# A planned two-layer graph attention kernel: other landing times and another search in its planner, and W2's column sums without score columns

## The chip, the cores and the metric

The kernel runs on one core of a Trainium2 chip. The metric is the device time of one execution in microseconds (us). A core has five engines that matter here: TensorE (PE, matrix products into PSUM), VectorE (DVE), ScalarE (ACT), GpSimd (POOL) and SyncE (SP). Each works off its own list of instructions in order; an instruction that has to wait for a semaphore holds up everything behind it on the same engine. In this kernel SP issues the plain and transposing DMAs, and POOL issues the DMAs that add to their destination.

## The reference

For 32 graphs of 512 nodes with 512 features, the reference normalizes x, applies two graph attention layers with the same 0/1 adjacency mask, and adds the result to x. The first layer has 4 heads of 256 features and an ELU, the second has one head of 512.

```python
def gat_layer(x, mask, W, a_src, a_dst, bias, concat):
    xl = (x @ W).reshape(B, N, H, F)
    asrc = jnp.einsum('bnhf,hf->bnh', xl, a_src)
    adst = jnp.einsum('bnhf,hf->bnh', xl, a_dst)
    e = jax.nn.leaky_relu(asrc[:, :, None, :] + adst[:, None, :, :], 0.2)
    e = jnp.where(mask[..., None], e, -1e9)
    attn = jax.nn.softmax(e, axis=1)
    out = jnp.einsum('bsdh,bshf->bdhf', attn, xl)
    return (out.reshape(B, N, H * F) if concat else out.mean(axis=2)) + bias

h = jnp.maximum(_layernorm(x, axis=-1), 0.0)
h1 = jax.nn.elu(gat_layer(h, mask, W1, att_src1, att_dst1, b1, concat=True))
out = x + gat_layer(h1, mask, W2, att_src2, att_dst2, b2, concat=False)
```

## The kernel before

**The work of one batch.** A batch (one graph) goes through five stages. `load` and `norm` bring x in and normalize it; `norm_turn` transposes it into `ht`. `project1` multiplies `ht` by W1 into `xl`, with two extra columns per head that hold the two attention scores of each node. For each head, `Soft.columns`, `Soft.first` and `Soft.second` make the attention weights: the scores are turned and sent as a row to DRAM and back to all partitions (tiles `as`, DRAM `das`), ScalarE makes the leaky ReLU and the exponentials (tile `l`), VectorE the masked minimum, a second row goes the same way (tiles `rr`, DRAM `drr`), VectorE builds `p` from it, POOL adds the mask to `p` with an accumulating DMA (`p<-dm`), and ScalarE takes the exponential of `p`. `gather1` multiplies by `xl` into `h1`; `elu` follows. `project2` multiplies `h1` by W2 into `xl2`, and `gather2` multiplies by the second layer's `p` and adds x. Products use a seven-product scheme for two-by-two blocks (as Strassen's), so VectorE also makes sums and differences of blocks (`hs`, `t`, `hl`, in-place ones), and each of seven products is emptied from its PSUM bank by ScalarE (a copy) or VectorE (an add or subtract) before the next product may be put into the bank.

**The order of the work.** Nothing is emitted when these functions run. Each call adds a job to a `Program`: its engine, a cost in us, the tiles it reads and writes, and for DMAs a size in us of transfer. `Program.order` then plans. TensorE's jobs keep the order in which the code adds them. For the other four engines a simulation (`forwards`) takes, whenever an engine is free, the ready job with the lowest rank. A DMA is held to have landed `DMA_LEAD` + its size (divided by a speed if both queues transfer) + `DMA_TAIL` after its issue; `DMA_TAIL` is 1.2 us for both queues. A DMA is not issued while more than `AHEAD` = 3.5 us of transfers are queued. Twelve rounds of a backwards and a forwards simulation give ranks, and the best round is kept. Then, for stretches of 80 TensorE jobs (`STRETCH`), `sooner` lowers the rank of jobs that stand in the chain of causes before a TensorE gap, in one of six `WAYS` (how far back, how strongly), and the whole program is simulated again; a try is kept if TensorE comes to a job 40 beyond the stretch sooner. Each engine's jobs are emitted in the planned order, which is then fixed.

**W2 and the second bias.** Layer 1's output is kept one higher than ELU gives it, so the column sums of W2 are taken from the bias once. `weights2` is called in the code after the first batches' projections. It loads W2 as four blocks (`w2_sb`, 512 KB each), b1, b2 and the two score vectors of layer 2 (spread over all partitions, into two `t` tiles); the four W2 loads read the key of `ht`'s first tile, so they wait for the last job that wrote it, which at that place is batch 1's `norm_turn`. Then VectorE multiplies every row of W2 with each score vector and sums: 2 vectors x 4 blocks x 4 = 32 products, whose sums land in `part`, and four small adds put them into column 256 of each block (`w2s`). `bias2` multiplies a tile of ones by the blocks, 257 columns wide (two PSUM banks of eight program-level matmuls each, 32 matmul instructions in the trace), subtracts the banks from `b2_sb`, takes `c2` (the scores' offset) from column 256, and sets that column to 0. On TensorE the job of `bias2` stands between batch 1's `project1` and batch 0's gathers. `b2_sb` is read by `project2` as the first content of its banks, `c2` by `scores_2`.

In the trace, W1 and W2 both show as `w_sb`, the DVE jobs have line L449, the ACT jobs L446, the matmuls L463, the DMAs of SP L452 (L658 and L717 for the two kinds of transposes), those of POOL L457. DVE accumulations show as a product and a short read of the accumulator.

Of the kernel before, what the change touches and what calls it, by code (L numbers as in the profile page):

```python
# [3 lines left out]

# [6 lines left out]
F32 = mybir.dt.float32  # L11
# [4 lines left out]
OP = mybir.AluOpType  # L16
# [3 lines left out]
P = 128  # L20
# [5 lines left out]
def rows_of(ap, n):  # L26

    return bass.AP(tensor=ap.tensor, offset=ap.offset, ap=[[0, n], [1, ap.shape[-1]]])
# [31 lines left out]
        self.free.append(key[1])  # L60


class Program:


# [4 lines left out]

    CROSS, SAME = 0.15, 0.07
    PAIRS = {("PE", "ACT"): 0.21, ("PE", "DVE"): 0.21, ("DVE", "POOL"): 0.58, ("POOL", "DVE"): 0.4}
    DMA_LEAD, DMA_TAIL, AHEAD = {"SP": 0.6, "POOL": 0.75}, {"SP": 1.2, "POOL": 1.2}, 3.5
    ALONE = {"SP": 1.0, "POOL": 1.0}
    SHARED = {0: {"SP": 0.44, "POOL": 0.62}, 1: {"SP": 0.3, "POOL": 0.62}}
    TURN = 0.95
# [90 lines left out]
                release(j, lambda s: t + jobs[j][1] + self.latency(j, s))  # L167
        return start, done, cause

    def sooner(self, rank, start, cause, span, gain, first, last):  # L170


        jobs, lost, free = self.jobs, {}, 0.0
        for i, j in enumerate(self.tensor):
            gap, free = start[j] - free, start[j] + jobs[j][1]
            if not first <= i < last:
                continue
            d = cause[j]
            while gap > 0.05 and d is not None and start[j] - start[d] < span:
                lost[d] = max(lost.get(d, 0.0), gap)  # L180
                d = cause[d]
        return [r - gain * lost.get(j, 0.0) for j, r in enumerate(rank)]

    WAYS = tuple((span, gain) for span in (60.0, 25.0) for gain in (2.0, 0.7, 6.0))
    STRETCH = 80

    def backwards(self, rank):

# [60 lines left out]
    def order(self):  # L249
        jobs = self.jobs  # L250
        n = len(jobs)
        self.after = [[] for _ in range(n)]
        for j, job in enumerate(jobs):
            for d in job[2]:
                self.after[d].append(j)

        need, pe = [0.0] * n, None
        for j in reversed(range(n)):
            later = self.DMA_LEAD.get(jobs[j][0], 0.0) + self.DMA_TAIL.get(jobs[j][0], 0.0) + (jobs[j][4] or 0.0)
            need[j] = max(  # L260
                (
                    need[s] + jobs[s][1] + (later if jobs[j][4] is not None else self.latency(j, s))
                    for s in self.after[j]
                ),
                default=0.0,
            )
            if jobs[j][0] == "PE":
                if pe is not None:
                    need[j] = max(need[j], need[pe] + jobs[pe][1])
                pe = j  # L270
        best, self.tried = None, []
        self.tensor = [j for j in range(n) if jobs[j][0] == "PE"]

        def look(rank):
            nonlocal best
            start, done, cause = self.forwards(rank)
            end = max(start[j] + jobs[j][1] for j in range(n))
            self.tried.append(end)
            if best is None or end < best[0]:
                best = end, start, done, cause, rank  # L280
            return start, cause

        rank = need
        for _ in range(self.ROUNDS):
            back = self.backwards(rank)
            rank = [-back[j] - jobs[j][1] for j in range(n)]
            start, cause = look(rank)
            rank = [-start[j] - jobs[j][1] for j in range(n)]

        _, start, done, cause, rank = best  # L290
        n_pe = len(self.tensor)
        for first in range(0, n_pe, self.STRETCH):
            last = min(first + self.STRETCH, n_pe)
            goal = self.tensor[min(last + self.STRETCH // 2, n_pe - 1)]
            tries = deque(self.WAYS)
            while tries:
                new = self.sooner(rank, start, cause, *tries.popleft(), first, last)
                if new == rank:
                    break
                result = self.forwards(new)  # L300
                if result[0][goal] < start[goal] - 0.01:
                    rank, (start, done, cause) = new, result
                    tries = deque(self.WAYS)
                    self.tried.append(max(start[j] + jobs[j][1] for j in range(n)))
        self.start, self.late = start, rank
        return done

    def emit(self):
        for j in self.order():
# [4 lines left out]
def tile_gat(  # L314
# [36 lines left out]
    nc = tc.nc  # L351
# [10 lines left out]
    KH = FT // 2  # L362
    W2H = DO // 2 + 1
    assert N == 512 and D == 512 and DO == D and FH == 256 and H == 4

    sbuf = ctx.enter_context(tc.tile_pool(name="sbuf", bufs=1))
# [22 lines left out]
    AT = {(0, 0): 0, (0, 1): 6, (1, 0): 1, (1, 1): 2}  # L389
    b1_sb = sbuf.tile([P, FT], F32, name="b1_sb")  # L390
    b2_sb = sbuf.tile([P, 2, W2H], F32, name="b2_sb")
    c2 = sbuf.tile([P, 2], F32, name="c2")
    w1_low = sbuf.tile([P, 3, W], F32, name="w1_low")
    hl = sbuf.tile([P, 3, P], F32, name="hl")
    later = sbuf.tile([P, 2, W], F32, name="later")
# [52 lines left out]
    def dve(cost, reads, writes, f, *a, **k):  # L448
        prog.add("DVE", cost, reads, writes, lambda: f(*a, **k))  # L449

    def dma(size, reads, writes, to, at, cost=0.4):
        prog.add("SP", cost, reads, writes, lambda: nc.sync.dma_start(to, at), size)  # L452
# [100 lines left out]
                prog.alias(vk + (u, c), [vk + ("v", a, j) for a in range(2) for j in range(H // 2)])  # L553
        ps_.give(vk)

    def weights2():

        for (r, c), ix in AT.items():
            dma(
                1.5, [("ht", 0, 0)], [("w2", ix)], w2_sb[:, ix, :, :M],  # L560
                w2[r * HF // 2 : (r + 1) * HF // 2, c * DO // 2 : (c + 1) * DO // 2].rearrange(
                    "(k p) f -> p k f", p=P
                ),
            )
        dma(0.1, (), ["b1"], b1_sb, b1.rearrange("(c p) -> p c", p=P))
        dve(TINY, ["b1"], ["b1"], nc.vector.tensor_scalar_add, b1_sb, b1_sb, 1.0)
        dve(0.3, (), ["b2"], nc.vector.memset, b2_sb, 0.0)
        for c in range(2):
            dma(
                0.4, (), ["b2"], b2_sb[:, c, :M],  # L570
                bass.AP(tensor=b2.tensor, offset=b2.offset + c * M, ap=[[0, P], [1, M]]),
            )
        for a, v in enumerate((as2, ad2)):
            lk, bc = ts_.take()
            dma(0.75, (), [lk], bc, rows_of(v[0], P))
            for (r, c), ix in AT.items():
                for k in range(KH):
                    jk, junk = xrs.take()
                    dve(
                        0.4, [lk, ("w2", ix)], [("part", a, r, c, k), jk],  # L580
                        nc.vector.scalar_tensor_tensor,
                        junk[:, : DO // 2], w2_sb[:, ix, k, :M], 1.0,
                        bc[:, c * DO // 2 : (c + 1) * DO // 2], op0=OP.mult, op1=OP.mult,
                        accum_out=part[:, a, r * KH + k, c : c + 1],
                    )
                    xrs.give(jk)
            ts_.give(lk)
        for a in range(2):
            for r in range(2):
                g = part[:, a, r * KH : (r + 1) * KH, :]  # L590
                dve(
                    TINY, [("part", a, r, c, k) for c in range(2) for k in range(KH)],
                    [("w2s", AT[r, a])], nc.vector.tensor_add,
                    w2_sb[:, AT[r, a], :, M:], g[:, :, 0:1], g[:, :, 1:2],
                )


    def bias2():

        ok, ones = ts_.take()  # L600
        ones = ones[:, :P]
        dve(0.2, (), [ok], nc.vector.memset, ones, 1.0)
        for c in range(2):
            bk, bt = banks.take(W2H)
            pe(
                [ok, *(k for r in range(2) for k in (("w2", AT[r, c]), ("w2s", AT[r, c])))],
                [bk], 2 * KH * W2H / 593,
                [
                    (mm, (bt[:, :W2H], ones, w2_sb[:, AT[r, c], k, :]),
                     dict(start=(r == 0 and k == 0), stop=(r == 1 and k == KH - 1)))  # L610
                    for r in range(2) for k in range(KH)
                ],
            )
            dve(ADD, [bk, "b2"], ["b2"], nc.vector.tensor_sub, b2_sb[:, c], b2_sb[:, c], bt[:, :W2H])
            banks.give(bk)
        dve(TINY, ["b2"], ["c2"], nc.vector.tensor_copy, c2, b2_sb[:, :, M])
        dve(0.34, ["b2"], ["b2"], nc.vector.tensor_sub, b2_sb[:, 1], b2_sb[:, 1], b2_sb[:, 0])
        dve(TINY, ["b2", "c2"], ["b2"], nc.vector.memset, b2_sb[:, :, M:], 0.0)
        ts_.give(ok)

    XT, MASK, MASKT, ST = {}, {}, {}, {}
# [789 lines left out]
    def run(products):  # L1411
        for _ in products:
            pass
# [18 lines left out]
    scores1()  # L1432
    masks(0)
    given = [zs.take() for _ in range(2)]
    run(project1_first(given))
    load(1)
    norm(1)
# [143 lines left out]
```

## Time and profile before

| what | value |
|---|---|
| time, median of 3 runs (lowest to highest) | 2785.98 us (2781.57 to 2786.17) |
| the profiled execution's own time | 2789.86 us |
| span of that execution, first to last instruction | 2788.1 us |
| mean granted TensorE clock | 0.999 |
| first matmul starts | 10.6 us |
| ACT busy | 2244.9 us (81%) |
| POOL busy | 328.0 us (12%) |
| DMA: bytes moved, mean rate | 502.09 MB, 180 GB/s |
| accumulating DMAs p<-dm | 314, 512 KB each |
| relays as<-das and rr<-drr | 96 and 161 |

The profile page comes from one execution. Busy time counts an engine's instructions from start to end; the ends of matmuls are modelled. A wait is put down to the engine, or the landing of a DMA, whose semaphore event came last before the waiting instruction started. In the rows below, a row of a timeline gives the start in us, the time in us that the merged instructions took together, the engine, the line, the operation, what is written and read, the shape, how many instructions were merged, and in brackets the idle time before and who ended it. A row of waits gives who waited for whom, the total in us, how often, and the longest in us. A row of a stage gives its time, then for PE, PEld (weight loads), DVE, ACT and POOL the busy time and the number of instructions, then the granted clock, the DMA engines' busy share and GB/s.

### The profile page before, as it was taken

What the parts mean: (1) busy time and instruction counts of PE and PEld (TensorE: products, weight loads), DVE (VectorE), ACT (ScalarE), POOL (GpSimd) and SP (SyncE); (2) the same over time, 40 slices, a digit from 0 to 9 for tenths busy, and PEclk for the clock granted to TensorE, in tenths of its full rate; (3) what the DMA queues carried; (4) which work ended last, traced back from release to release, by engine and by line L of the source; (5) the groups of instructions that cost most, each with busy time, mean ns of one, the idle gap of its engine ahead of it and who ended that gap; (6) DMA issues with size and microseconds to landing.
All of it is one profiled execution on the core that took longest, in us unless ns stands there. A gap on an engine that the chain in (4) does not pass through costs nothing. (4 is left out here: it accounts for less than half of the span.)

```text
span 2788.1 us, 41716 instructions
## 1 busy us (share of the span) xinstructions
PE 2747.0 (99%) x12490; PEld 2361.8 (85%) x12490; DVE 2626.0 (94%) x6857; ACT 2244.9 (81%) x4751; POOL 328.0 (12%) x356
## 2 busy tenths in 40 slices
PE   8999999999999999999999999999999999999999
PEld 7688888888888888888888888888888888888877
DVE  8989999999999999999999999999999999999986
ACT  5978887888888888978788887878878788788873
POOL 0100111101111101111011111111110111101110
PEclk9999999999999999999999999999999999999999
DMA  7766767676776677666676766776666876677663
GB/s 237 154 170 176 205 168 191 183 184 177 192 187 173 182 183 200 172 173 182 167 200 172 192 179 185 167 196 184 171 188 171 197 178 170 177 184 197 167 167 106
DMA packets 375861, 502.09 MB, mean 180 GB/s; under 512 B 222804, under 2 KB 227668, under 8 KB 375636
## 3 DMA queue, kind: packets, MB, share of 16 engines
q1 hardware_dynamic: 329844, 332.68, 42.9%
q0 software_dynamic: 45792, 166.74, 25.2%
q8 instruction: 100, 1.64, 0.2%
q14 instruction: 125, 1.02, 0.1%
HBM read 316.41 MB, written 51.31 MB: 132 GB/s over the span
## 5 line engine op out<-in xcount | busy, mean ns | idle before, releaser
L463 PE MATMUL mm<-w_sb,hs 128*128 128x257 f32 (+2 forms) x3032 | 697.5, 381 | 3.8 <-DVE hs L449 1.9
L463 PEld LDWEIGHTS mm<-w_sb,hs 128*128 128x128 f32 x3032 | 574.5, 190 | 91.4 <-DVE hs L449 3.1
L457 POOL DMA_DIRECT2D p<-dm x314 | 275.6, 878 | 2306.4 <-DVE p L449 1212.1
L446 ACT ACTIVATE l<-as,z 128x512 f32<-128x512 f32 x640 | 439.9, 716 | 111.6 <-DMA as<-das 110.4
L446 ACT ACTIVATE l<-l,low 128x512 f32<-128x512 f32 x640 | 457.5, 718 | 34.4 <-DVE low L449 32.2
L446 ACT ACTIVATE p<-p,z 128x512 f32<-128x512 f32 (+1 forms) x636 | 430.9, 715 | 56.3 <-DMA p<-dm 45.8
L463 PE MATMUL mm<-w_sb,h 128*128 128x257 f32 x2056 | 469.4, 380 | 3.8 <-ACT w_sb L446 3.8
L463 PE MATMUL mm<-p,xl 128*128 128x256 f32 (+1 forms) x1984 | 468.0, 384 | 1.5 <-ACT h L446 1.5
L449 DVE SCALAR_TENSOR_TENSOR p<-rr,z 128x512 f32<-128x512 f32 (+1 forms) x636 | 447.6, 738 | 16.2 <-DMA rr<-drr 15.9
L449 DVE CUSTOM_DVE_ANT_1 l<-l,mt 128x512 f32<-128x512 f32 x640 | 426.1, 681 | 21.4 <-ACT l L446 20.6
L463 PEld LDWEIGHTS mm<-w_sb,h 128*128 128x128 f32 x2056 | 389.7, 190 | 62.5 <-ACT w_sb L446 4.2
L463 PE MATMUL mm<-w_sb,ht 128*128 128x258 f32 x1802 | 428.9, 385 | 13.8 <-DVE xl L449 12.6
L463 PEld LDWEIGHTS mm<-p,xl 128*128 128x128 f32 x1984 | 377.1, 190 | 62.0 <-issue 6.0
L463 PEld LDWEIGHTS mm<-w_sb,ht 128*128 128x128 f32 x1802 | 336.9, 190 | 80.2 <-DVE xl L449 29.7
L446 ACT ACTIVATE h<-mm,b_sb 128x256 f32<-128x256 f32 (+1 forms) x504 | 232.0, 474 | 144.7 <-PE mm L463 142.7
L446 ACT ACTIVATE xl<-mm 128x258 f32<-128x258 f32 (+2 forms) x686 | 253.8, 379 | 50.6 <-PE mm L463 47.8
L449 DVE TENSOR_TENSOR xl<-xl,mm 128x258 f32<-128x258 f32 (+1 forms) x526 | 212.4, 414 | 38.0 <-PE mm L463 29.2
L463 PE MATMUL mm<-t,hs 128*128 128x256 f32 x992 | 225.5, 379 | 0.1
L463 PEld LDWEIGHTS mm<-t,hs 128*128 128x128 f32 x992 | 188.2, 190 | 26.6 <-ACT h L446 0.6
L446 ACT ACTIVATE xr<-h 128x512 f32<-128x512 f32 x256 | 159.2, 627 | 40.8 <-DVE h L449 39.2
L449 DVE TENSOR_TENSOR t<-mm,t 128x256 f32<-128x256 f32 (+1 forms) x424 | 171.7, 416 | 15.3 <-PE mm L463 13.7
L463 PE MATMUL mm<-xl,p 128*128 128x256 f32 (+1 forms) x752 | 179.3, 387 | 0.0
(130 smaller groups left out, 3448.2 us busy)
## 6 DMA issues: line engine op xcount, KB each, us to landing
p<-dm POOLq DMA_DIRECT2D x314, 512.0 KB, 5.6
rr<-drr SPq DMA_DIRECT2D x159, 512.0 KB
x<-in_x_dram SPq DMA_DIRECT2D x129, 256.0 KB
adj<-in_adj_dram SPq DMA_DIRECT2D x128, 256.0 KB
as<-das SPq DMA_DIRECT2D x64, 512.0 KB
t<-in_x_dram SPq DMA_DIRECT2D x124, 256.0 KB
out_dram<-t SPq DMA_DIRECT2D x124, 256.0 KB
dm<-m SPq DMA_DIRECT2D x64, 256.0 KB
```

The costliest lines, as they stand in the source:

```text
L446: prog.add("ACT", cost, reads, writes, lambda: nc.scalar.activation(*a, **k))
L449: prog.add("DVE", cost, reads, writes, lambda: f(*a, **k))
L457: lambda: nc.gpsimd.dma_start(to, at, accum_op=OP.add), size,
L463: f(*a, **k)
```

## The change

It has three parts.

1. `DMA_TAIL` is 2.7 us in place of 1.2 us. In the final search, `tail` gives this value only while TensorE's position is past the first 150 jobs (`HEAD`) and before the last 150 (`REAR`); elsewhere it gives `ENDS` = 1.2. The twelve rounds before use 2.7 throughout.
2. The stretches and `sooner` are replaced. `better` keeps states of the simulation (`Run`, with `copy`, `resume` and `go`) at marks every 20 TensorE jobs. It walks along TensorE's planned jobs to the next gap over 0.1 us, and makes up to 100 tries for it: the first sixteen go through the `WAYS` (four spans, four gains), the others multiply each job's step by a random number. A try starts from a mark that lies before the first job whose rank it moves, runs to 80 jobs past the gap, and is kept if TensorE is there more than 0.02 us sooner. The rules of the simulation itself are the same.
3. `weights2` is split. `load2`, with the loads, is called before batch 1's `load`, so the W2 loads wait for batch 0's `norm_turn`. `weights2` keeps the 32 products and the four adds, with a planner's cost of 0.36 in place of 0.4. `bias2` multiplies only the 256 columns of W2; `c2` is made from its banks by four VectorE products with the score vectors and one small add. The copy to `c2` and the last memset are gone.

```diff
-    DMA_LEAD, DMA_TAIL, AHEAD = {"SP": 0.6, "POOL": 0.75}, {"SP": 1.2, "POOL": 1.2}, 3.5
+    DMA_LEAD, DMA_TAIL, AHEAD = {"SP": 0.6, "POOL": 0.75}, {"SP": 2.7, "POOL": 2.7}, 3.5
...
-    WAYS = tuple((span, gain) for span in (60.0, 25.0) for gain in (2.0, 0.7, 6.0))
-    STRETCH = 80
+    WAYS = tuple((span, gain) for span in (60.0, 25.0, 100.0, 12.0) for gain in (2.0, 0.7, 6.0, 15.0))
...
+    MARK, SIGHT, TRIES, BACK = 20, 80, 100, 5.0
+    ENDS, HEAD, REAR = 1.2, 150, 150
+
+    def inner(self, at):
+        return self.HEAD <= at < len(self.tensor) - self.REAR
+
+    def tail(self, which, at):
+        return self.DMA_TAIL[which] if self.inner(at) else self.ENDS
+
+    def better(self, rank):
...
+            goal = min(i + self.SIGHT, end)
+            aim, won = start[tensor[goal - 1]], False
+            for k in range(self.TRIES):
+                span, gain = self.WAYS[k % len(self.WAYS)]
...
+                rough = k >= len(self.WAYS)
+                new = rank[:]
+                first = float("inf")
+                for d, v in lost.items():
+                    if jobs[d][0] != "PE":
+                        new[d] -= gain * v * (chance.random() * 2 if rough else 1.0)
+                        first = min(first, start[d])
+                m = max(q for q in range(len(marks)) if q == 0 or start[tensor[marks[q].at - 1]] < first - self.BACK)
+                run = marks[m].copy()
+                run.resume(new)
+                if run.go(new, goal) < aim - 0.02:
+                    rank, won = new, True
+                    del marks[m + 1 :]
+                    extend()
+                    break
...
-    def weights2():
+    ROWS2 = []
+
+    def load2():
         for (r, c), ix in AT.items():
             dma(1.5, [("ht", 0, 0)], [("w2", ix)], w2_sb[:, ix, :, :M], ...)
...
+        for v in (as2, ad2):
+            lk, bc = ts_.take()
+            dma(0.75, (), [lk], bc, rows_of(v[0], P))
+            ROWS2.append((lk, bc))
...
+    def weights2():
+        for a, (lk, bc) in enumerate(ROWS2):
...
-            bk, bt = banks.take(W2H)
+            bk, bt = banks.take(M)
             pe(
-                [ok, *(k for r in range(2) for k in (("w2", AT[r, c]), ("w2s", AT[r, c])))],
-                [bk], 2 * KH * W2H / 593,
+                [ok, *(("w2", AT[r, c]) for r in range(2))], [bk], 2 * KH * M / 593,
...
-            dve(ADD, [bk, "b2"], ["b2"], nc.vector.tensor_sub, b2_sb[:, c], b2_sb[:, c], bt[:, :W2H])
+            for a, (lk, bc) in enumerate(ROWS2):
+                jk, junk = xrs.take()
+                dve(
+                    0.36, [bk, lk], [("cols", a, c), jk], nc.vector.scalar_tensor_tensor,
+                    junk[:, :M], bt[:, :M], -1.0, bc[:, c * M : (c + 1) * M], op0=OP.mult, op1=OP.mult,
+                    accum_out=cols2[:, a, c : c + 1],
+                )
+                xrs.give(jk)
+            dve(0.335, [bk, "b2"], ["b2"], nc.vector.tensor_sub, b2_sb[:, c, :M], b2_sb[:, c, :M], bt[:, :M])
             banks.give(bk)
-        dve(TINY, ["b2"], ["c2"], nc.vector.tensor_copy, c2, b2_sb[:, :, M])
-        dve(0.34, ["b2"], ["b2"], nc.vector.tensor_sub, b2_sb[:, 1], b2_sb[:, 1], b2_sb[:, 0])
-        dve(TINY, ["b2", "c2"], ["b2"], nc.vector.memset, b2_sb[:, :, M:], 0.0)
+        dve(TINY, [("cols", a, c) for a in range(2) for c in range(2)], ["c2"], nc.vector.tensor_add, c2, cols2[:, :, 0], cols2[:, :, 1])
+        dve(0.335, ["b2"], ["b2"], nc.vector.tensor_sub, b2_sb[:, 1], b2_sb[:, 1], b2_sb[:, 0])
...
     scores1()
     masks(0)
     given = [zs.take() for _ in range(2)]
+    load2()
     run(project1_first(given))
     load(1)
     norm(1)
```

## The prediction

> **What bounds the kernel.** I read the page first, then the list of who waited for whom, the timeline around each long wait, and last the times by stage.
>
> ```profile
> PE 2747.0 (99%) x12490; PEld 2361.8 (85%) x12490; DVE 2626.0 (94%) x6857; ACT 2244.9 (81%) x4751; POOL 328.0 (12%) x356
> ```
>
> TensorE is busy for 99% of the span; VectorE, at 94%, is close behind. A change that leaves the matmuls alone can win only what TensorE stands idle. I took that idle time from the trace by start-to-start distances: an undisturbed matmul of 258 columns follows the one before by 0.217 us, so whatever lies beyond columns/1186 us is lost. TensorE starts at 10.6 us and its last matmul ends 3.9 us before the span does. Between them stand 2722 us of matmuls and 51 us of loss; 2.4 us of that is rounding of the pace. The rest: 3.9 us up to 20 us, 8.6 from 20 to 173 us, 28.3 from 173 to 2628 us, 8.0 after. Each stall also costs 0.10 us at the next matmul, whose weights were not loaded ahead; that is in these sums.
>
> ```profile
> PE mm L463 <- DVE xl L449: 12.8, 18, 2.1
> PE mm L463 <- ACT x L446: 10.9, 2, 10.6
> PE mm L463 <- ACT w_sb L446: 3.8, 1, 3.8
> PE mm L463 <- ACT h L446: 3.6, 3, 2.1
> ```
>
> Columns: total us, times, longest us. The second line is the start. In the others TensorE waits until VectorE or ScalarE has emptied a PSUM bank. Why such an emptying is late shows in the 12 us before the stall at 1206.4 us, the longest of the middle (waits there, then the engines' rows):
>
> ```profile
> ACT l L446 <- DMA as<-das: 4.8, 1, 4.8
> DVE hs L449 <- ACT p L446: 1.8, 1, 1.8
> PE mm L463 <- DVE xl L449: 1.6, 1, 1.6
> ...
> 1195.05 1.95 ACT L446 ACTIVATE l<-as,z 128x512 f32<-128x512 f32 x3 [4.83 <-DMA as<-das]
> ...
> 1205.32 0.69 DVE L449 TENSOR_TENSOR hs<-p 128x512 f32<-128x512 f32 x1 [1.78 <-ACT p L446]
> 1205.93 0.41 DVE L449 TENSOR_TENSOR xl<-xl,mm 128x258 f32<-128x258 f32 x1
> ```
>
> A broadcast of scores landed late. ScalarE, in order, stood 4.83 us before it and then worked off a backlog; its exponential of p came late; VectorE waited 1.78 us for that with the bank's subtraction (xl<-xl,mm) queued behind, and TensorE behind that. Of nineteen middle stalls over 0.5 us (19.7 us together) I followed fifteen; fourteen have a ScalarE wait for a landing (as, p or the transposes x<-adj) in the 12 us before. ScalarE has some 89 such waits in these 2455 us, so by chance 12 us would hold one in about 35% of cases: the landings are no bystanders.
>
> **Part 1, longer landings.** The planner's DMA_TAIL goes from 1.2 to 2.7 us where the TensorE position lies between job 150 and the last 150, by my count of jobs 173 to about 2628 us; outside, 1.2 stays in the final search. No instruction is added or removed, only order. From the trace's landing events I took the time from the end of the issue to the last arrival: as<-das median 4.8 us, p<-dm 4.8, rr<-drr 4.3. Less the planner's lead and size (0.6+1.92 us for as and rr, 0.75+2.3 for p), the part beyond the old 1.2 us is exceeded by 75% of the as landings, 73% of rr, 62% of p and 45% of x<-adj; beyond 2.7 us by 29, 24, 32 and 17%. The planner also slows transfers that share, so these shares overstate how often it is surprised, but the ratio stands: some 60% of late landings come inside the new allowance.
>
> The rule that speaks against it: the Trainium skill, "DMA: Bandwidth & Descriptors", "Anatomy of one DMA — SWDGE (gpsimd) path", gives a POOL-issued DMA a fixed cost near 2.0 us plus its bytes over 436 GB/s, 3.2 us for 512 KB as an estimate. Lead and tail before (0.75+1.2) meet that; after (0.75+2.7) they overshoot by 1.5 us, which would give part 1 no gain. The row decides:
>
> ```profile
> p<-dm POOLq DMA_DIRECT2D x314, 512.0 KB, 5.6
> ```
>
> 5.6 us is the median from issue to landing, with 7.9 us for the slowest tenth in the middle. I take 60%.
>
> **Part 2, the search.** Before: stretches of 80 jobs, six ways each. After: every planned gap over 0.1 us gets up to 100 tries, restarted from marks every 20 jobs. It mends waits that the plan sees, and cannot see the chip's late ones. For middle stalls the bounds are -10 us (a new order crowds VectorE, busy for 767 of the 800 us from 400 us on) and +28.3 us. I take half, 14.2 us: 60% for causes inside the allowance, less a sixth for new stalls made by earlier-ranked feeders. In the last 160 us the tail is still 1.2; there p<-dm landed 8.3 us after its issue, so the plan is as blind as before. I take 30% of 8.0, 2.4 us, between -3 and 8. For the start I take nothing (bounds -1 to 2): loads and normalization stay as they are.
>
> A stall in front shows a second cost:
>
> ```profile
> 144.87 1.13 PE L463 MATMUL mm<-p,hs 128*128 128x256 f32 x4 [2.06 <-ACT h L446]
> 145.84 3.37 PE L463 MATMUL mm<-p,xl 128*128 128x256 f32 x8
> ...
> 133.15 3.62 PE L463 MATMUL mm<-p,xl 128*128 128x256 f32 x16
> ```
>
> After 2.06 us idle, eight matmuls took 3.37 us where undisturbed sixteen take 3.62; the granted clock was 0.5 for 3.41 us there, and again after the 3.8 us wait at 2685 us. The skill, "TensorE: Matmul & The Clock Gate", "What's actually happening", asks for a whole idle window of about 3.4 us before half clock. By that rule the stall at 144.9 is worth 2.3 us; by the rows 4.0 (2.2 idle, 0.1 restart, 1.7 half clock). I count 4.0. An equally long wait at 72.3 us was not followed by it, so it cannot be counted for every wait.
>
> **Part 3, W2 without score columns.** In bias2 the two ones-by-W2 products ran 32 matmuls of 257 columns; 256 columns save 32/1186, 0.03 us. But they also needed the score columns, 32 VectorE products and four adds:
>
> ```profile
> 71.81 0.42 DVE L449 TENSOR_TENSOR xl<-xl,mm 128x258 f32<-128x258 f32 x1
> 72.14 0.42 DVE L449 SCALAR_TENSOR_TENSOR xr<-w_sb,t 128x256 f32<-128x256 f32 x1
> 72.28 0.73 PEld L463 LDWEIGHTS mm<-w_sb,ht 128*128 128x128 f32 x4 [2.48 <-DVE xl L449]
> ...
> 65.00:80.00 15.00, 12.43 (x57) 10.37 (x57) 15.00 (x67) 9.74 (x22) 2.95 (x4) 1.00 0.66 176
> ```
>
> VectorE is full from 65 to 80 us (third column, 15.00 of 15.00) and ran score products at 0.345 us each ahead of the subtraction that TensorE waited 2.1 us for; with restart this stall is 2.4 us. The need for the columns moves to the sums of W2, at 94.8 us, where only 2.45 of 29 us are idle from 80 to 109. So the cover is W2's earlier load: its four 512 KB DMAs hung on batch 1's turned activations and were issued at 46.2 to 48.9 us; now they hang on batch 0's, ready at 13.2 us. Of the 11 us of products, 5 fit the idle time of VectorE from 15 to 65 us. If that cover fails, the stall comes back near 95 to 109 us, at most 2.4 us. On SP's queue they may pass what was issued between 14 and 46 us: batch 1's x, six mask loads, four mask transposes, three mask stores and the first score relay. Four issues at 0.4 us and 6 us of planned transfer could delay those, at most by one transfer of 1.5 us on TensorE's path, but SP stands empty from 38.1 to 43.8 us. The score rows, b1 and b2 were already issued at 16 to 28 us. Two t buffers are held longer; but for the ones tile nothing takes t before 122 us. Added: four products of a bank with a score row, 4 x 0.36 us (nearest row 0.345), one tiny add against a copy and a memset, 1.3 us of VectorE; needed by the seeds at 109 us and the scores at 132.9, against 88.8 us before, hidden. Without that cover, 1.3 us. I take 2.3 us gained, between -1.5 and 2.4, and 40% of the remaining 5.9 us around 49 to 145 us (stalls at 65.5, 103.5 and 144.9, old tail), 2.4 us.
>
> **Sum.** 2.3 + 2.4 + 14.2 + 2.4 = 21.3 us. Span 2788.1 to 2766.8; the profiled run took 2789.9, 1.8 more, and the median of the runs is 2786.0, 3.9 below it. I apply the saving to the median: **2765 us**.
>
> **Rivals.** *Nearly all stalls go*: 85% of the middle (24), 7 in front, 6 at the end, 37 us, 2749. For it: VectorE itself waited 29 us for TensorE's banks, so there is slack to place. Against it: a quarter of landings exceed even 2.7 us. *The reordering does little*: landings vary more than any constant; the stalls move elsewhere. Only the front's 4 us and a tenth of the middle remain, 7 us, 2779. For it: from 173 to 1200 us the old tail lost only 5.5 us, from 1200 to 1400 it lost 6.7, the same program. *Slower*: feeders of every landing are ranked 1.5 us earlier, so VectorE takes row maxima and p sums ahead of bank subtractions. The place is the project1 stage of the 31 rounds; at one subtraction (0.42 us) and its restart (0.10) more waited for in two places each, 31 x 1.04 = 32 us against the 21 saved: 2797. It decides from 0.69 us per round on. Against it: a search that ends only when TensorE's planned gaps cannot be closed pays for such a delay.
>
> **Numbers.** Chances 0.60 forecast (own range 2755 to 2776), 0.13 nearly all, 0.17 little, 0.10 slower. 0.2%, 5.6 us, is about what a measurement of this kernel can tell from no change. Faster: 0.60+0.13+0.11; same: 0.06 of the third case and 0.01 of the last; slower 0.09. The range, 2750 to 2784, leaves out half of the fullest mending and most of the slower case.
>
> **What would show it.** TensorE's waits for VectorE's xl fall from 12.8 to about 6 us; the sum from 173 to 2628 us from 28 to about 14; no stall at 72 us, W2's DMAs before 40 us; ScalarE's 110 us of waits for as<-das well down. The forecast is wrong if ScalarE waits as long for landings as before, if new xl stalls of over 0.7 us per round stand in the middle, or if the half clock appears there.

## The result

The changed kernel takes 2774.0 us (median; 2769.4 to 2779.2) against 2787.0 us for the kernel before on the same chip. The ratio is 0.9949, with a 95% interval of 0.9936 to 0.9963: 0.51% faster, some 14 us (13 us by the two medians). The forecast was 21 us. In a second set of runs the ratio was 0.9946 (0.9931 to 0.9961). The profiled execution shown here has a span of 2775.8 us, 12.3 less than before; a second profile of the same kernel has 2770.2.

The first part of the page of the kernel after:

```profile
PE 2740.8 (99%) x12490; PEld 2367.3 (85%) x12490; DVE 2627.0 (95%) x6864; ACT 2238.7 (81%) x4751; POOL 322.7 (12%) x356
```

There are as many matmuls, and VectorE works 1.0 us longer. What fell is the time that TensorE loses between matmuls: counted as in the prediction, with the time before the first matmul, it went from 59.4 to 47.3 us, 12.1 less. (The page's busy time of TensorE, whose ends are modelled, cannot show this split.) Who TensorE waited for, in the kernel after:

```profile
PE mm L644 <- ACT x L627: 12.7, 1, 12.7
PE mm L644 <- ACT p L627: 9.3, 4, 4.8
PE mm L644 <- DVE hs L630: 2.8, 2, 2.6
PE mm L644 <- ACT h L627: 2.6, 2, 2.1
PE mm L644 <- DVE xl L630: 1.8, 1, 1.8
```

The waits for VectorE's bank subtractions (xl) fell from 12.8 us in 18 waits to 1.8 us in one. In their place stand few, longer waits for ScalarE's exponential of p. What ScalarE itself waited for, before and after:

```profile
ACT l L446 <- DMA as<-das: 110.4, 55, 5.5
ACT p L446 <- DMA p<-dm: 45.8, 38, 5.1
```

```profile
ACT l L627 <- DMA as<-das: 24.7, 13, 5.8
ACT adj L627 <- DMA x<-adj: 9.9, 4, 5.6
...
ACT p L627 <- DMA p<-dm: 9.0, 7, 2.1
```

ScalarE comes to the score rows before they have landed in 13 cases, where it did in 55. The stage around the column sums of W2, after (columns as before: time, then PE, PEld, DVE, ACT, POOL):

```profile
65.00:80.00 15.00, 15.00 (x67) 12.33 (x66) 14.99 (x65) 13.67 (x28) 3.73 (x4) 1.00 1.04 234
```

TensorE has 15.00 us of work in these 15 us (12.43 before). The timeline of SP and TensorE after shows why it need not wait:

```profile
17.73 2.96 SPq L633 DMA_DIRECT2D w_sb<-in_L_gnn_W_dram  x4
```

```profile
71.42 7.08 PE L644 MATMUL mm<-w_sb,t 128*128 128x256 f32 x32
```

W2's loads go out at 17.7 to 20.7 us (46.2 to 48.9 before), and the 32 matmuls of the column sums follow the ones before without a gap.

TensorE's loss, counted from start-to-start distances as in the prediction, in the one profiled execution of each kernel (us; 20 to 173 us is called the front, 173 to 2628 us the middle, with its number of stalls, where losses at matmuls in direct succession are one stall; "as" is ScalarE's total wait for as<-das; parts 1, 2, 3 are the long landings, the new search, the W2 edit):

| kernel | first matmul | to 20 us | 20 to 173 | middle | after 2628 | as | ratio (95%) |
|---|---|---|---|---|---|---|---|
| before | 10.6 | 3.9 | 8.6 | 28.3 (71) | 8.0 | 110 | 1 |
| after: 1, 2, 3 | 12.7 | 2.4 | 9.2 | 19.4 (25) | 3.6 | 25 | 0.9949 (0.9936 to 0.9963) |
| after_again: 1, 2, 3 | 12.1 | 2.4 | 1.8 | 21.6 (33) | 3.8 | 22 | 0.9946 (0.9931 to 0.9961) |
| planner_only: 1, 2 | 9.9 | 4.0 | 8.8 | 19.6 (39) | 1.8 | 12 | 0.9949 (0.9937 to 0.9961) |
| tail_only: 1 | 9.5 | 4.2 | 8.8 | 32.5 (44) | 3.5 | 16 | 0.9997 (0.9983 to 1.0010) |
| old_search: 1, 3 | 10.7 | 3.7 | 16.2 | 23.6 (63) | 6.6 | 28 | 1.0025 (1.0008 to 1.0043) |
| tail12: 2, 3 | 10.3 | 5.1 | 2.6 | 38.0 (72) | 7.7 | 96 | 1.0016 (1.0003 to 1.0028) |
| w2_only: 3 | 12.3 | 1.5 | 8.4 | 35.6 (60) | 5.3 | 109 | 1.0034 (1.0022 to 1.0046) |

One execution's losses scatter by some us, as the two profiles of one kernel show in the front (9.2 and 1.8); the ratios rest on 5 to 22 runs of each kernel. Every row is one plan. Part 2 alone, without parts 1 and 3, was not run.

### The profile page after: what moved, and what is told of

Its sections match the earlier page's. It is cut to its first block, busy times and chain, and to the rows that moved or that the text cites. A ratio compares the mean times of both kernels' runs of the same rounds, so it can differ in the third digit from the quotient of the medians.

```text
span 2775.8 us, 41905 instructions
## 1 busy us (share of the span) xinstructions
PE 2740.8 (99%) x12490; PEld 2367.3 (85%) x12490; DVE 2627.0 (95%) x6864; ACT 2238.7 (81%) x4751; POOL 322.7 (12%) x356
## 4 chain that ended last, share of the span: by engine, by line
PE 91%; DVE 3%; DMA 3%; issue 2%; ACT 1%; POOL 0%; SPq 0%; POOLq 0%; DVEq 0%; ACTq 0%
PE mm L644 91%; DMA x<-adj 1%; DVE l L630 1%; DMA p<-dm 1%; DVE p L630 1%; DVE xl L630 0%; DVE hs L630 0%; DVE h L630 0%; DVE w_sb L630 0%; DMA mt<-m 0%; POOL p L638 0%; DMA w_sb<-in_L_gnn_W_dram 0%; ACT x L627 0%; DVE t L630 0%; ACT ht L627 0%
## 5 line engine op out<-in xcount | busy, mean ns | idle before, releaser
L627 ACT ACTIVATE p<-p,z 128x512 f32<-128x512 f32 (+1 forms) x636 | 421.9, 716 | 24.5 <-DVE p L630 9.8
L644 PEld LDWEIGHTS mm<-p,xl 128*128 128x128 f32 x1984 | 377.6, 191 | 70.3 <-ACT p L627 12.3
L644 PE MATMUL mm<-w_sb,ht 128*128 128x258 f32 x1802 | 421.7, 383 | 2.2 <-DVE xl L630 1.8
```

What stands on the lines that cost most here:

```text
L627: prog.add("ACT", cost, reads, writes, lambda: nc.scalar.activation(*a, **k))
```

## The experiments

**The W2 edit alone.** The planner of before with all of part 3 as shown in "The change"; of its edit:

```diff
-    def weights2():
+    ROWS2 = []
+
+    def load2():
...
-                        0.4, [lk, ("w2", ix)], [("part", a, r, c, k), jk],
+                        0.36, [lk, ("w2", ix)], [("part", a, r, c, k), jk],
...
+    load2()
     run(project1_first(given))
     load(1)
```

> Part 3 alone: the planner of before (tail 1.2 us, stretches of 80 jobs, six ways), with W2's loads moved up and the column sums made without the score columns. My theory (late landings are the middle's loss): the stall at 72 us goes, the middle from 173 to 2628 us keeps 20 to 30 us of loss, and the time is 2 to 4 us under before (ratio 0.9985 to 0.9993). If part 3 had carried the change's gain, the ratio would be near 0.995. If any new plan of the old planner only rolls the dice, the ratio lies anywhere from 0.997 to 1.003 and the middle's stalls stand at other places.

Measured: 2792.7 us, ratio 1.0034, slower. The stall at 72 us is gone, but others stand ahead of it. TensorE's timeline in that run:

```profile
53.47 1.14 PE L464 MATMUL mm<-w_sb,hs 128*128 128x258 f32 x4 [1.96 <-ACT xl L447]
...
60.04 1.23 PE L464 MATMUL mm<-w_sb,hl 128*128 128x258 f32 x2 [2.82 <-ACT later L447]
```

Waits of 2.0 and 2.8 us for ScalarE's emptying of banks have taken its place (with restart and half clock 2.2 and 4.5 us of loss), the first matmul starts 1.7 us later, and the middle, with the same old landings, lost 35.6 us. The wait that part 3 removes came back elsewhere. Every change of the jobs makes another plan, which would do this; that it is the plan, and not a cost of part 3 under the old search, was not tested (no second plan of this kernel was run).

**The new search without the long landings.** The kernel after with

```diff
-    DMA_LEAD, DMA_TAIL, AHEAD = {"SP": 0.6, "POOL": 0.75}, {"SP": 2.7, "POOL": 2.7}, 3.5
+    DMA_LEAD, DMA_TAIL, AHEAD = {"SP": 0.6, "POOL": 0.75}, {"SP": 1.2, "POOL": 1.2}, 3.5
```

> Parts 2 and 3 without part 1: the new search and the W2 edit, but landings planned with 1.2 us throughout. Theory landings: the many stalls under 2 us come back in the middle, 25 us or more, ScalarE's waits for as<-das are near 100 us again, and the ratio to before is 0.997 to 1.000. Rival search: most of the gain stays, ratio 0.994 to 0.996, ScalarE's waits for as<-das are under 50 us.

Measured: 2790.6 us, ratio 1.0016; no gain is left. ScalarE's waits in that run:

```profile
ACT l L627 <- DMA as<-das: 95.5, 43, 5.6
ACT p L627 <- DMA p<-dm: 30.0, 33, 3.6
```

TensorE's waits for the bank subtractions are there as before (before: 12.8, 18, 2.1):

```profile
PE mm L644 <- DVE xl L630: 10.0, 17, 2.3
```

The front is good (2.6 us of loss from 20 to 173 us), and the middle is not: 72 stalls, 38.0 us. In this plan a hundred tries with landings planned too early did not help on the chip. The rival that the new search carries the gain whatever the landings falls with it, as far as one plan goes.

**The long landings without the new search, with and without part 3.** The planner of before, with the landing chosen by TensorE's position; the old search otherwise unchanged:

```diff
-                release(j, lambda s: event + self.DMA_TAIL[which])
+                late = self.DMA_TAIL[which] if even or 150 <= n_pe - len(tensor) < n_pe - 150 else 1.2
+                release(j, lambda s: event + late)
```

(`DMA_TAIL` is 2.7; `even` is set in the twelve rounds.) With part 3:

> Parts 1 and 3 without part 2: the old search of stretches with six ways, landings planned with 2.7 us between job 150 and the last 150 and 1.2 us outside, and the W2 edit. Theory landings: most of the gain stays, ratio 0.995 to 0.997, ScalarE's waits for as<-das below 40 us. Rival search: waits that the plan sees are left standing, the middle loses 25 us or more, ratio 0.998 to 1.003.

Measured: 2793.7 us, ratio 1.0025. Without it:

> Part 1 alone: the old search and the W2 code of before, landings planned with 2.7 us between job 150 and the last 150 and 1.2 us outside. With part 3 as well this was 0.25% slower than before, with a middle loss of 23.6 us and 16 us of stalls between 20 and 142 us. If longer landings without the new search win in the middle and lose in front, the middle loses 15 to 25 us, ScalarE's waits for as<-das are under 40 us, the front from 20 to 173 us loses over 10 us, and the ratio is 0.998 to 1.003. If the front's loss came from part 3's early loads under the old planner, the front loses under 8 us and the ratio is 0.994 to 0.997.

Measured: 2785.9 us, ratio 0.9997. ScalarE's waits in that last run:

```profile
ACT adj L449 <- DMA x<-adj: 20.4, 7, 5.5
ACT l L449 <- DMA as<-das: 16.0, 14, 4.0
```

And TensorE's, with xl no longer among those shown:

```profile
PE mm L466 <- ACT p L449: 15.6, 6, 5.5
PE mm L466 <- ACT x L449: 9.5, 1, 9.5
PE mm L466 <- DVE w_sb L452: 5.2, 2, 2.9
```

Most of ScalarE's wait for score rows is gone here too, and TensorE's waits for xl in the middle are down to 0.6 us (10.7 before; 1.3 with part 3, and at most 1.8 with all three parts), so this part of the mechanism belongs to part 1 alone. But it buys nothing by itself: without part 3, 32.5 us are lost in the middle, 20.0 of them in four stalls of 2.7 to 8.7 us, and 7.1 us in two stalls at 73.0 and 79.7 us; with part 3, 16.2 us from 20 to 173 us. My guess in the expectation, that the front would lose over 10 us in both, was wrong for the run without part 3 (8.8 us).

**Both, without part 3.** The changed planner on the W2 code of before:

> Parts 1 and 2 without part 3: the changed planner on the code of before for W2 and its column sums. My step said that part 3 is worth 2.3 us; the run with part 3 alone was 0.34% slower than before, so that value is in doubt. If part 3 is worth 2.3 us in itself, the ratio is 0.9955 to 0.996, and a stall of 1 us or more stands before the column sums near 72 us. If the new search plans around the score columns anyway, there is no such stall, and the ratio is 0.9935 to 0.9955, the same as with all three parts.

Measured: 2774.5 us, ratio 0.9949, the same as with all three parts. TensorE's waits there:

```profile
PE mm L643 <- ACT p L626: 5.7, 5, 2.1
PE mm L643 <- ACT xl L626: 2.9, 3, 2.2
PE mm L643 <- DVE w_sb L629: 2.0, 2, 1.4
```

Both expectations were half right: TensorE does wait before the column sums (the last row; 2.6 us of loss in two stalls at 76.2 and 81.3 us), and the time is the same all the same. (The longest wait for xl, 2.2 us at 68.0 us, was followed by half clock and cost 4.1 us; it stands ahead of the sums.) In the run with part 1 alone the two column sums waited 2.5 and 4.6 us. In no kernel with part 3 does a stall over 0.5 us begin between 64 and 80 us, though two have a long one shortly ahead (4.5 us at 60.0 in w2_only, 6.1 at 61.3 in turn_slow, an experiment below). So part 3 removes a wait of 2.4 to 7.1 us at its place. In the total it cannot be seen: the intervals of the two ratios reach 0.12 to 0.14% to each side, and 2.3 us are 0.08%.

**The changed kernel again.**

> The changed kernel as it is, for a second trace. If its three large stalls of the middle (7.6 us at 1077, 4.4 us at 1520, 2.3 us at 735) are accidents of one execution, they are absent or elsewhere here, the middle loses 8 to 14 us and the profiled run is near 2770 us. If the plan makes them, they stand at the same places within 10 us and the middle loses 19 us again. Ratio 0.993 to 0.9965 either way.

Measured: ratio 0.9946, span 2770.2 us. The stalls of 7.6 and 2.3 us came back (6.4 us at 1075, 3.3 us at 728), the one at 1520 us did not, and 4.4 us at 984 to 987 us were new. So the plan seems to make some of them. How one comes about, in the first profile:

```profile
1060.94 1.71 SPq L913 DMA_TRANSPOSE x<-adj  x1
1061.13 0.87 POOL L638 DMA_DIRECT2D p<-dm  x1 [0.60 <-PE mm L644]
...
1074.55 1.06 ACT L627 ACTIVATE adj<-x 128x1024 uint16<-128x1024 uint16 x1 [5.61 <-DMA x<-adj]
1075.51 2.54 ACT L627 ACTIVATE p<-p,z 128x512 f32<-128x512 f32 x4
...
1076.86 0.69 DVE L630 TENSOR_TENSOR t<-p,t 128x512 f32<-128x512 f32 x1 [7.10 <-ACT p L627]
...
1077.49 0.80 PE L644 MATMUL mm<-p,xl 128*128 128x256 f32 x1 [4.85 <-ACT p L627]
```

A transposing DMA and an accumulating one were issued 0.2 us apart, and by the landing events both took over 12 us, counted from issue. ScalarE stood 5.61 us before the transpose, with the exponentials of p queued behind it, and TensorE behind those. In both profiles together (landings taken from the landing events), nine of ten middle stalls over 1.5 us (a stretch at half clock counted by itself) follow, within 25 us, a transpose x<-adj that landed more than 9 us after its issue. Before, there was one such transpose in the middle. With landings of 2.7 us there were 6 to 16 in each trace, with the old search too (8 in old_search, 16 in tail_only, whose four long stalls all follow one); with 1.2 us there were 1 to 4, with the new search too (4 in tail12). So they come with part 1, not with the search.

**Another seed.**

```diff
-        chance = Random(1)
+        chance = Random(2)
```

> The changed kernel with another seed of its random tries (2 in place of 1), so another plan by the same rules. If the gain is a property of the rules, the ratio is 0.9925 to 0.997, ScalarE's waits for as<-das are 20 to 35 us, and large stalls of the middle stand at other places than 730, 984 and 1076 us. If the gain was a lucky plan, the ratio is 0.998 to 1.003.

Measured: 2773.2 us, ratio 0.9944 (0.9932 to 0.9956); ScalarE's waits for as<-das 15.0 us; the only middle stall over 1.5 us at 744 us (7.1 us), behind a late transpose again; 14.9 us were lost in the front. The gain does not hang on one lucky plan: the two seeds differ by less than their intervals.

**Landings of 2.0 us.** The same line as above, with 2.0 in place of 2.7.

> The changed kernel with landings planned 2.0 us after the transfer in the middle in place of 2.7 (1.2 gave a ratio of 1.0016 with the same search). Theory landings: in between, ScalarE's waits for as<-das 40 to 75 us, ratio 0.996 to 1.000. If 1.2 was only an unlucky plan, the ratio is as with 2.7, 0.993 to 0.9965, with ScalarE's waits for as<-das below 35 us.

Measured: 2769.4 us, ratio 0.9936 (0.9924 to 0.9948). ScalarE's waits in that run:

```profile
ACT l L627 <- DMA as<-das: 44.5, 32, 4.5
ACT p L627 <- DMA p<-dm: 17.2, 15, 4.3
```

As a theory of ScalarE's waits this was right (44.5 us, between 96 and 25). As a theory of the time it was not: the whole gain is there at 2.0 us. What 2.7 us removes of ScalarE's waits beyond that did not show in the time.

**The x loads first.** The first matmul of the kernel after starts 2.1 us later than before. SP's and TensorE's rows at its start:

```profile
2.13 0.69 SPq L633 DMA_DIRECT2D w_sb<-in_L_gnn_W_dram  x1
2.86 0.59 SPq L633 DMA_DIRECT2D x<-in_x_dram  x1
```

```profile
12.67 1.12 PE L644 MATMUL mm<-identf,x 128*128 128x128 f32 x4 [12.67 <-ACT x L627]
```

The fourth x tile went out behind a block of W1. One rule in `better` puts the four loads first:

```diff
+        rank = [-1e9 if j < 4 else r for j, r in enumerate(rank)]
         marks = [Run(self)]
```

> The changed kernel with one rule more: the four loads of the first x tiles go ahead of everything on SP. In the changed kernel the fourth x tile is loaded behind W1 blocks, and the first matmul starts at 12.4 to 12.7 us against 10.6 before. If that order is the cause, the first matmul starts at 10.5 to 11 us and the time falls by 1.5 to 2 us, ratio 0.9925 to 0.9945. If the start is set by VectorE's products behind W1's landing, it stays above 12 us.

Measured: the first matmul at 10.0 us, but ratio 0.9956 (0.9939 to 0.9972), no different from the kernel after; single runs went from 2764 to 2783 us, and the profiled one was the fastest of them. With 2.0 us as well:

> The changed kernel with landings planned 2.0 us after the transfer and the first four x loads ahead of everything on SP. The first matmul starts at 10 to 11 us (12.2 with 2.0 us alone). If a start 2 us earlier is kept to the end, the ratio is 0.9915 to 0.994; if the plan gives it back in the next 60 us, 0.993 to 0.996.

Measured: **2762.3 us, ratio 0.9910** (0.9891 to 0.9928), with no middle stall over 1.5 us. This beats both kernels. (The profiled execution is the slowest of the six, 2766.4 us; nine transposes landed late in its middle, and no long stall followed.) The earlier start, 1.4 us against 2.0 us alone, is a fifth of the 7 us between the two medians; where the rest comes from was not tested. TensorE's first row:

```profile
10.56 2.82 PE L645 MATMUL mm<-identf,x 128*128 128x128 f32 x12 [10.56 <-ACT x L628]
```

**The colliding pair.** Two tries against late transposes, both with 2.0 us. One plans the pair slower:

```diff
-    SHARED = {0: {"SP": 0.44, "POOL": 0.62}, 1: {"SP": 0.3, "POOL": 0.62}}
+    SHARED = {0: {"SP": 0.44, "POOL": 0.62}, 1: {"SP": 0.15, "POOL": 0.3}}
```

> The changed kernel with landings planned 2.0 us after the transfer, and with transfers planned at 0.15 (SP) and 0.3 (POOL) of full speed, in place of 0.3 and 0.62, while a transposing DMA of SP runs beside an accumulating DMA of POOL. In the traces of the new planner nearly all middle stalls over 1.5 us follow a transpose x<-adj that landed over 9 us after its issue. If the planner's too fast speeds for this pair are what leaves them, no middle stall over 1.5 us follows such a transpose, and the ratio is 0.990 to 0.993. If the late transposes come from elsewhere, or the slower plan costs as much, the ratio stays 0.993 to 0.996 with stalls of over 1.5 us left.

Measured: 2800.8 us, ratio 1.0044 (1.0028 to 1.0060). No transpose x<-adj of the middle landed over 9 us late (the slowest 7.7 us), and only 3 of all were issued within 0.5 us of an accumulating DMA (20 with 2.0 us alone). So with few such pairs the late transposes were gone; but the whole plan is another, and this run does not set the pair's share apart. It lost 43 us in the middle, with TensorE waiting 9.8 us for VectorE's xl and 6.6 us for ScalarE's p; long stalls (2.1 to 4.5 us) stand there without a late transpose. The other holds the one kind back, in the simulation, while the other transfers:

```diff
                 if q in self.wires:
                     t = max(t, self.now + self.behind[q] - program.AHEAD)
+                    other = "POOL" if q == "SP" else "SP"
+                    if self.wires[other]:
...
+                        if turns:
+                            t = max(t, self.now + self.behind[other])
```

> The changed kernel with landings planned 2.0 us after the transfer, and with one rule more in the simulation: a transposing DMA is not issued while an accumulating DMA transfers, nor the reverse. If the pair running together is what makes a transpose land over 9 us late, fewer than 3 such transposes are left in the middle (12 with parts 1 and 2 alone, 3 with 2.0 us), the accumulating DMAs' slowest tenth falls under 7.5 us, and the ratio is 0.990 to 0.993. If they are late for another cause, as many are left, and the ratio is 0.993 to 0.997.

Measured: 2784.9 us, ratio 1.0000 (0.9983 to 1.0017). Ten transposes were still issued within 0.5 us of an accumulating DMA and five of the middle landed over 9 us after issue: the order in the plan did not keep them apart on the chip. Of these five only one was issued in such a pair, and the other nine pairs were not late. So the pair as such is not the whole cause, and what else makes a transpose late stays open. Why this plan gains nothing was not followed up.

## Why the prediction was right, and where it was not

The direction and the range held; the size, 21 us, was half again the measured 14, which lies about midway between the forecast and the rival "the reordering does little" (7 us, 2779). The range holds that rival too, so the number alone does not tell the two apart; the waits do.

**What bounds the kernel** held: the same matmuls, and TensorE's loss fell by 12.1 and 17.7 us where the span fell by 12.3 and 17.9 us, in the two profiles.

**Part 1, landings.** The chain was right: late score row, ScalarE in order, VectorE, bank, TensorE. In every kernel with 2.7 us TensorE's waits for xl in the middle nearly went (10.7 us before, at most 2.2 with 2.7 us); the other kernels with 1.2 us kept them (9.7 and 15.3). ScalarE's wait for as<-das fell by 78% in the page and by two thirds or more in every kernel with 2.7 us, with either search and either W2 code. The weighing of the rule of the Trainium skill ("DMA: Bandwidth & Descriptors", "Anatomy of one DMA — SWDGE (gpsimd) path", fixed cost near 2.0 us) against the row was right in sign: planned at 1.2 us, the same search gained nothing, in the one plan run. But 2.7 us was not needed; 2.0 us gained as much.

**Part 2, half of 28.3 us.** This step failed in size: the middle kept 19.4 and 21.6 us, so 9 and 7 us went, not 14. The short stalls went further than the "60% inside the allowance": those of 0.3 to 1.5 us fell from 26 (18.5 us) to 2 and 9 (0.6 and 4.5 us). The "sixth for new stalls" was too small. Stalls of 1.5 us and over grew from 5.3 us to 16.3 and 14.9 us, nine of ten of them (counted as above) behind a late transpose. The prediction took late landings as given; the number of late transposes depends on the order. It did not grow with the number of pairs within 0.5 us of an accumulating DMA, which fell (19 before, 15 and 16 after), so how the order brings it about stays open.

**The sum itself** treated the parts as terms to be added. They are not: part 1 alone 0.9997, part 2 with part 3 1.0016, parts 1 and 2 0.9949. In the plans that were run, neither the landings nor the search gained without the other: six plans with both gained 0.4 to 0.9%, and none of the four without one of them gained. Two more plans with both, but with another rule in the simulation (turn_slow, turn_held), did not gain either, so a plan can still lose what the two give. Why part 1 alone gains nothing, its trace shows: the short stalls fell (17 of 9.9 us where there were 26 of 18.5), and four long ones behind late transposes took it back (20.0 us). (With part 3 as well the short ones did not fall: 30 of 18.6 us.) What the new search adds is seen in the loss only: 19.6 us in the middle against 32.5 with the same landings and W2 code, 10.3 against 20.0 of it in stalls of 1.5 us and over, with late transposes still there (12). How it does this the runs do not show.

**Part 3, 2.3 us** is not confirmed as a term of the time. The wait at the column sums did go and W2 was loaded early; but the parts without it measure the same, within intervals wider than 2.3 us. With the old search it was slower by some 0.3% both times (1.0034 against 1; 1.0025 against 0.9997), and lost that at different places: in the middle alone (35.6 us against 28.3), in the front beside part 1 (16.2 against 8.8). What I missed is that an edit of the jobs replans everything. That these 0.3% are scatter from plan to plan fits the differing places, but no second plan of the old search was run.

**The start, nothing**, was wrong in its reason: the loads did not stay as they were. The first matmul came 2.1 us later, while the loss up to 20 us fell by 1.5. **The last 160 us, 2.4 us**: 4.4 and 4.2 us were gained, although the planned landing is the same there. It is not shown to be the search: 7.7 us were lost there with the new search and 1.2 us, 3.5 us with the old search and 2.7 us. **The front's other stalls, 2.4 us**: total loss from 20 to 173 us went from 8.6 to 9.2 and 1.8, so nothing can be read from one profile.

**The half clock.** The prediction named half clock in the middle as a sign that the forecast is wrong, and the sign came, though the time stayed in the range: the granted clock was 0.5 for 6.8 us from 1075.7 us and for 3.4 us from 1519.4 us in the first profile, for 3.4 us from 986.3 and from 1075.1 us in the second; before, there was none in the middle. It followed the long stalls and made them longer: 4.7 us of idle and restart at 1074.5 us in the second profile cost 1.7 us more at half clock. So the few long stalls gave back part of what the many short ones had cost.

**The rival that ends slower** did not happen for the change, but four experiments ended slower, by another path than mine. It asked for two more late subtractions in each of 31 rounds; the waits for xl in the middle were 3 to 20 in these four (17 before). Stalls of 1.5 us and over made 13.3 to 15.0 us of the middle's loss in w2_only, tail12 and turn_slow (5.3 before), at other places in each; old_search lost 16.2 us in three front stalls, two of them with half clock.

## What to carry to other kernels

In a planned kernel an edit's price is not read from the stall it removes: compare several plans (seeds, constants) before crediting a term, and judge constants and search together, since here neither gained without the other. A planner's landing time may sit near the median of the trace: 2.0 us did what 2.7 us did, 1.2 us gained nothing, and the medians of the trace before, less the planner's lead and size, are about 1.7 to 2.3 us for as, rr and p. And look at what a better order leaves: with the many short waits gone, a few late transfers set the rest of the loss.

## What the runs showed of the hardware

A transposing DMA x<-adj that SP issued within 0.5 us of an accumulating DMA p<-dm landed after 6.7 us (median; slowest tenth 11.7 us or more), over 170 cases in the traces of ten executions (before, after twice, w2_only, tail12, old_search, planner_only, x_first, seed2, tail20); the other 1030 took 4.2 us (slowest tenth 6.8). The accumulating DMA of such a pair took 6.1 us (slowest tenth 11.3) against 5.6 (7.7). With the pairs nearly gone (turn_slow), the transposes over 9 us were gone too. But the pair is neither needed nor enough: of the 75 transposes over 9 us in these ten traces 36 were in such a pair, and 134 pairs were not late. Closer to a condition is an accumulating DMA in flight when the transpose is issued: 72 of 590 such transposes took over 9 us, and 3 of the other 610. This is counted, not tried; why the two land later together no run shows.
